# Between two attentions: another fixed order for routing and shared expert, and a shorter first lead in layer 1

## The chip, the cores and the metric

One Trainium2 chip, one of its cores. The time is the device time of one execution of the whole program in microseconds (us), the median of several runs; lower is better. The engines of the core run side by side, each through its own queue in order: TensorE (PE; PEld is its weight load), VectorE (DVE), ScalarE (ACT), GpSimd (POOL) and SyncE (SP, which issues most transfers).

## The reference, cut to what matters

2048 tokens of 128 channels, fp32, two layers, each with a modulated layer norm ahead of its attention and of its second half.

```python
h = layernorm(x) * (1 + ca) + sa
x = x + ga * attention0(h)            # 16 heads of 8, every token sees all 2048
h = layernorm(x) * (1 + cb) + sb
# 16 experts, the best one for each token, its score through a sigmoid,
# and a shared expert of width 512 for all tokens
x = x + gb * (down_e(silu(gate_e(s*h)) * up_e(s*h)) + shared_down(silu(h@G) * (h@U)))
h = layernorm(x) * (1 + ca1) + sa1
x = x + ga1 * attention1(h)           # 8 query heads of 16, one key/value head, causal
h = layernorm(x) * (1 + cb1) + sb1
x = x + gb1 * sigmoid(mix(h) @ Wr) * (relu(mix(h) @ Wk)**2 @ Wv)
```

## The kernel before, in words

Tokens are cut into 16 tiles of 128 and four blocks of 512 (`b` 0 to 3). `x` stays in SBUF with tokens on the partitions; the normed `h1` and `h2` lie transposed, channels on the partitions.

**Attention** (`attention`, both layers) works in units: one block of queries and one group of four heads, eight units in all. Each unit has two passes. The *first pass* computes scores for query tiles only to find the row maxima (TensorE L379, DVE L383, or L388 on the causal diagonal); a step is one query tile, one key block and two heads. `largest` packs the negated maxima, and `turn` transposes them (L412, copy L413). The *second pass* computes scores transposed (L444), adds the shift (L450, layer 1 only), takes the exponential on ScalarE (L454), clears what lies above the diagonal on POOL (L457) and weighs the values (L470). Three score tiles (`ps_s`) of two banks serve both passes. Two banks are left: one collects the weighed values, the other (`other_bank`) serves everything else, one piece after the other. `all_first` is a generator of all first-pass steps; `look_ahead(upto)` advances it. Before the first unit's second pass it runs `ends[0] + LEAD` steps, 16 in layer 1 (unit 0 and unit 1 have eight each), and afterwards stays eight steps and one unit's share ahead. In layer 1 the preparation of block b+1 (`ready1`: add the experts' rows and take moments, norm, turn, keys, values; then `project_q`, which ends in 16 transfers on SP's queue that stack the queries) starts at step 1 of the first unit of block b, one piece with each step. Unit 2 is the first that needs block 1. Within the attentions a planner sets each engine's order from its estimates of cost and from the order of the program.

**Between the attentions** (`last0` to `ordered.close()`) a manual schedule holds PE, DVE and ACT to the order in which the program issues their work; POOL and SP stay with the planner. `last0` returns the first list: the end of layer 0's attention for block 3 (`divide`, `turn_back`, `project`), the routing of block 3 (`moment`, `norm`, `turn`, `choose`, `place`, `turn_rows`, `send`; blocks 0 to 2 were routed inside the attention by the same `route`), the shared expert for block 0 in four slices (`up`, `times`, `down`, then `add`), and `tiles`, which computes on DVE which expert each of 31 slots of 128 rows belongs to. `send` scatters the scaled rows to DRAM with four indirect transfers from POOL (L759).

Then come the experts. SP reads the slots' start rows into registers and loads 31 tiles `xs` (L967) from what was scattered. Twelve *shared steps* (three blocks by four slices) remain: two products up (L941), Silu, a multiply (`acts`), and, one or two steps behind, a product down (L929). Eight *quads* of four slots run `gathered` (transpose xs, copy to `xsT`), `up_gate` (L1007, then `silu_up` into `acte`), `turn_act` (transpose, copy to `actT`) and `down` (L1020, then the multiply by gb L1024 and a write to `y_rows` from SP's queue, L1027). Pools: three `act` buffers shared by quads and shared steps, two `pg` tiles of two banks for `sg` and `gu`. Four shared steps run before the first quad, one in every second quad, four after. When all of `y_rows` is written, POOL gathers each token's row with 16 indirect transfers (L1044), addressed by `slot_i`.

At the head of layer 1 the pieces for block 0 follow all the shared work: add the gathered rows (L1062) and take moments, norm (L223), turn (L230, L231), keys (`stacked`, L265 to L267, `kS`), values and four stacked query products.

`moments` takes mean and variance per tile (L202, L203) and the inverse root by three Newton steps on DVE from a guess by shift (L205 to L217), so that ScalarE needs no other function table.

## Time and profile before

| | us |
|---|---|
| median of four runs (1273.35 to 1276.08) | 1275.21 |
| the profiled execution | 1275.1 |
| its span, first to last instruction | 1273.4 |
| layer 0's attention ends, the first list begins | about 817.5 |
| first shared up product of the experts' part | 847.18 |
| first quad's transposes | 857.74 |
| last quad's last product starts, then the last four shared steps | 901.84, 903.27 |
| last shared up product | 912.27 |
| first scores of layer 1 | 935.02 |
| first exponential of layer 1 | 962.43 |
| last product that weighs values | 1231.79 |

The mean granted TensorE clock is 0.935 of full. Over the span PE is busy 1168.1 us, DVE 946.9, ACT 774.1, POOL 95.2. All times below are from the start of the span. A stretch's row gives the busy time of each engine in it and how many instructions; a wait's row gives who waited, at which line, for whom, the sum, how often and the longest.

### The profile page before, as it was taken

How to read it: one execution, taken by the hardware profiler on the slowest of the kernel's cores; microseconds unless marked ns; L12 is line 12 of the kernel's file. 1: busy time of each engine (PE TensorE's matmuls, PEld its weight loads, DVE VectorE, ACT ScalarE, POOL GpSimd, SP SyncE). 2: the span in 40 equal slices, each digit the busy share in tenths (PEclk: the TensorE clock that was granted, in tenths of full speed). 3: DMA queues.
4: the chain of work that ended last, by engine and by line, in shares of the span. 5: the costliest groups of instructions: out<-in, count | busy, mean ns of one | idle time of the engine just before them, and what ended most of it. 6: DMA issues, size and time to landing. Idle time of an engine off the chain costs nothing.

```text
span 1273.4 us, 22384 instructions
## 1 busy us (share of the span) xinstructions
PE 1168.1 (92%) x9230; PEld 526.6 (41%) x9230; DVE 946.9 (74%) x1495; ACT 774.1 (61%) x843; POOL 95.2 (7%) x157
## 2 busy tenths in 40 slices
PE   5579999999999999999999999979768999999985
PEld 3233433443343343344344344447533444444432
DVE  3888898889889889898998881352467769888225
ACT  6107777777777777777777778613114435656763
POOL 2002000000000000000000000310311011100113
PEclk9658999999999999999999999979867779999998
DMA  4831010213122014010000000142201101000001
GB/s 120 114 47 34 2 52 1 68 33 86 52 68 68 2 47 121 2 51 2 2 2 2 2 1 6 40 124 60 58 11 33 34 1 35 1 2 1 1 2 33
DMA packets 63094, 45.22 MB, mean 36 GB/s; under 512 B 6608, under 2 KB 56912, under 8 KB 62480
## 3 DMA queue, kind: packets, MB, share of 16 engines
q1 hardware_dynamic: 60224, 40.37, 12.8%
q0 software_dynamic: 1024, 2.10, 0.6%
q10 hardware_dynamic: 1744, 1.32, 0.6%
q8 instruction: 73, 1.20, 0.4%
q14 instruction: 29, 0.24, 0.1%
HBM read 9.88 MB, written 21.95 MB: 25 GB/s over the span
## 4 chain that ended last, share of the span: by engine, by line
PE 81%; DVE 11%; ACT 4%; issue 2%; DMA 1%; POOL 1%; ACTq 0%; POOLq 0%; SPq 0%; DVEq 0%
PE a0bank L470 23%; PE a0p L444 17%; PE a0p L379 12%; PE a1bank L470 6%; PE a1p L444 4%; DVE a0mx L383 3%; PE a1p L379 2%; PE a1p L450 2%; DVE a1masked L388 2%; DVE a1mx L383 2%; PE sg L941 2%; ACT a0e L454 1%; PE gu L1007 1%; PE a1bank L265 1%; PE sum L929 1%
## 5 line engine op out<-in xcount | busy, mean ns | idle before, releaser
L383 DVE TENSOR_REDUCE a0mx<-a0p 128x2 f32<-128x1024 f32 x512 | 623.8, 1224 | 76.4 <-PE a0p L379 67.0
L454 ACT ACTIVATE a0e<-a0p 128x1024 f32<-128x1024 f32 x512 | 522.6, 1025 | 172.1 <-PE a0p L444 146.5
L470 PE MATMUL a0bank<-a0e,vA 128*32 128x256 f32 x4096 | 333.5, 392 | 0.2 <-ACT a0e L454 0.2
L379 PE MATMUL a0p<-kS,a0qS 64*128 64x512 f32 x1024 | 248.2, 481 | 24.7 <-DVE a0mx L383 13.4
L444 PE MATMUL a0p<-a0qS,kS 64*128 64x512 f32 x1024 | 260.5, 497 | 0.0
L454 ACT ACTIVATE a1e<-a1p 128x1024 f32<-128x1024 f32 (+3 forms) x160 | 143.2, 897 | 97.4 <-PE a1p L450 94.3
L444 PEld LDWEIGHTS a0p<-a0qS,kS 64*128 64x128 f32 x1024 | 97.3, 184 | 204.7 <-issue 128.4
L379 PEld LDWEIGHTS a0p<-kS,a0qS 64*128 64x128 f32 x1024 | 100.3, 192 | 109.3 <-ACT a0e L454 56.9
L470 PEld LDWEIGHTS a0bank<-a0e,vA 128*32 128x32 f32 x4096 | 86.4, 108 | 137.8 <-issue 124.7
L383 DVE TENSOR_REDUCE a1mx<-a1p 128x2 f32<-128x1024 f32 x96 | 115.8, 1222 | 28.6 <-PE a1p L379 27.7
L470 PE MATMUL a1bank<-a1e,vA 128*32 128x256 f32 (+1 forms) x1152 | 101.3, 385 | 2.3 <-POOL a1e L457 2.0
L444 PE MATMUL a1p<-a1qS,kS 64*128 64x512 f32 (+3 forms) x320 | 76.6, 471 | 2.8 <-DVE a1mx L388 0.9
L379 PE MATMUL a1p<-kS,a1qS 64*128 64x512 f32 (+3 forms) x320 | 68.8, 435 | 9.9 <-DVE a1mx L388 5.8
L388 DVE CUSTOM_DVE_ANT_0 a1masked<-a1p,later 128x128 f32<-128x128 f32 (+3 forms) x128 | 62.5, 488 | 12.1 <-PE a1p L379 7.1
L759 POOL DMA_INDIRECT sent<-hs,row_i x16 | 16.2, 1011 | 718.5 <-DVE ln11xn L223 689.9
L450 PE MATMUL a1p<-a1mT,a1ones 64*128 64x512 f32 (+3 forms) x320 | 62.1, 380 | 0.7 <-issue 0.7
L444 PEld LDWEIGHTS a1p<-a1qS,kS 64*128 64x128 f32 x320 | 31.6, 192 | 62.2 <-issue 33.2
L379 PEld LDWEIGHTS a1p<-kS,a1qS 64*128 64x128 f32 x320 | 33.1, 203 | 38.5 <-DVE a1mx L388 13.9
L457 POOL TENSOR_SCALAR_AFFINE_SELECT a1e<-a1e 128x256 f32<-128x256 f32 x64 | 26.3, 411 | 251.7 <-ACT a1e L454 251.7
L470 PEld LDWEIGHTS a1bank<-a1e,vA 128*32 128x32 f32 x1152 | 26.2, 109 | 45.8 <-issue 32.6
L413 ACT CAST a0mT<-a0bank 8x512 fp32r<-8x512 f32 x16 | 9.2, 576 | 45.1 <-PE a0bank L412 45.1
L450 PEld LDWEIGHTS a1p<-a1mT,a1ones 64*128 64x128 f32 x320 | 32.3, 197 | 2.3 <-issue 1.9
(342 smaller groups left out, 721.3 us busy)
## 6 DMA issues: line engine op xcount, KB each, us to landing
sent<-blank SPq DMA_DIRECT2D x68, 256.0 KB
kS<-a0qS SPq DMA_DIRECT2D x28, 128.0 KB
wgu_sb<-in_gate_up SPq DMA_DIRECT2D x1, 2048.0 KB
a0qS<-a0qh SPq DMA_DIRECT2D x62, 32.0 KB
a0qS<-a0ql SPq DMA_DIRECT2D x62, 32.0 KB
xs<-sent SPq DMA_DIRECT2D x31, 64.0 KB
y_rows<-y SPq DMA_DIRECT2D x7, 256.0 KB
a1qS<-a1qh SPq DMA_DIRECT2D x24, 64.0 KB
```

The source lines that it names most:

```text
L265: nc.tensor.matmul(ps, wS, h, start=True, stop=True)
L379: nc.tensor.matmul(ps[:, j, :n], qS[b][r:r + RT, st, i * P:(i + 1) * P], kS(st)[r:r + RT, kb * QB:kb * QB + n], start=True, stop=True)
L383: nc.vector.tensor_reduce(pm[:, i, 2 * pair:2 * pair + 2, kb], ps, AX.X, ALU.max)
L388: nc.vector.tensor_tensor_reduce(masked[:, :n], ps[:, j, :n], later[:, QB - n:], 1.0, LOWEST, ALU.add, ALU.max, pm[:, i, g, kb:kb + 1])
L444: nc.tensor.matmul(ps[:, j, q0:], kS(st)[r:r + RT, kt * P:(kt + 1) * P], qS[b][r:r + RT, st, q0:], start=True, stop=fused)
L450: nc.tensor.matmul(ps[:, j, q0:], ones[r:r + RT, g // S, :], shift[u][r:r + RT, q0:], start=False, stop=True)
L454: nc.scalar.activation(e[:, :, q0:], ps[:, :, q0:], AF.Exp, scale=scale)
L457: nc.gpsimd.affine_select(out=e[:, :, q0:q0 + P], in_=e[:, :, q0:q0 + P], compare_op=ALU.is_ge, fill=0.0, base=0, pattern=[[0, 2], [1, P]] ...
L470: nc.tensor.matmul(av[g * W:(g + 1) * W, c0:c1], vA(kt, grp * HG + g), held[kt, g // 2][:, g % 2, c0:c1], start=(kt == 0 and c0 == 0), sto ...
L759: nc.gpsimd.indirect_dma_start(out=sent[t], in_=hs[:, i, :], in_offset=None, out_offset=bass.IndirectOffsetOnAxis(ap=row_i.bitcast(U32)[:, ...
L929: nc.tensor.matmul(sums[b][:, i * P:(i + 1) * P], act[:, i * P:(i + 1) * P], wsd[:, k, :], start=(k == 0 and i == 0), stop=(k == NS - 1), ...
L941: nc.tensor.matmul(ps[:, j, :], w[:, k * P:(k + 1) * P], hT[:, b * QB:(b + 1) * QB], start=True, stop=True)
```

## The change

In `last0`, `divide` comes before the first `up`; Silu is a piece of its own; the moments' root is taken by ScalarE's Sqrt and a reciprocal on DVE, with `times(0)` between, and a one-column Sqrt ahead of it; `down(1)`, the rows and `place` follow `choose` directly; slices 2 and 3 come after `place`, their `times` and `down` after `tiles`; the running count (`ends_at`) is updated after `send`. In the experts' part three shared steps precede the quads (each with its down product as soon as one waits), three lie inside (quads 1, 3, 5) and six follow; each quad issues the next one's `gathered` first; `slot_i` is computed behind quad 2. At layer 1's head, add, norm and turn come after the last up product and the down product of the step before; the last multiply, keys, two queries, the last down product, values and two queries follow; the queries use the two-bank `pg` tiles; a one-column Exp is issued ahead. In layer 1's attention the first lead is 11 steps instead of 16 and grows back to eight ahead over unit 0's second pass, and block 1 is prepared from the first step of unit 1 (the other blocks as before).

```diff
...
-    def moments(b, name):
+    def moments(b, name, root=False, between=lambda: None):
...
         for i in range(TB):
             nc.vector.bn_stats(stats[:, i, :], x[:, b * TB + i, :])
             nc.vector.bn_aggr(mv[:, i, :], stats[:, i, :])
+        if root:
+            y = lnp.tile([P, TB], F32, name=name + "y", tag="y")
+            nc.scalar.activation(y, mv[:, :, 1], AF.Sqrt, bias=eps)
+            between()
+            nc.vector.reciprocal(y, y)
+            return mv, y
...
                             project_q(b + 1)
-                        if not fused and (grp, i) == (0, 1) and b + 1 < NB:
+                        if not fused and (grp, i) == (int(b == 0), 1 - int(b == 0)) and b + 1 < NB:
                             ready.extend(prepare(b + 1, other_bank))
                             ready.append(lambda b=b: project_q(b + 1))
...
-            look_ahead(ends[0] + LEAD)
+            short = 0 if fused else LEAD - 3
+            look_ahead(ends[0] + LEAD - short)
             for u in range(len(units)):
                 steps = second_pass(u)
                 size = ends[u] - (ends[u - 1] if u else 0)
                 more = ends[u + 1] - ends[u] if u + 1 < len(units) else 0
                 for n in range(1, size + 1):
                     next(steps)
-                    look_ahead(ends[u] + LEAD + more * n // size)
+                    lead = LEAD - (short * (size - n) // size if u == 0 else 0)
+                    look_ahead(ends[u] + lead + more * n // size)
                     if n == size:
                         next(steps, None)
...
             nc.vector.tensor_copy(row_i[:, ts], row[:, ts])
+            if not parts:
+                nc.vector.tensor_tensor(at[b + 1], at[b], ps[:, TB, :], ALU.add)
+            return ps
+
+        def ends_at(ps):
             nc.vector.tensor_tensor(at[b + 1], at[b], ps[:, TB, :], ALU.add)
...
         if parts:
-            return ([lambda: got.extend(moments(b, f"ln1{b}")),
+            return ([lambda between: got.extend(moments(b, f"ln1{b}", True, between)),
                      lambda: got.append(normal(b, f"ln1{b}", *got)),
                      lambda: turn_normal(bank(), got[2], h1[:, cols], m[:, 4:5], m[:, 3:4]),
-                     choose], place, turn_rows, send)
+                     choose], place, ends_at, turn_rows, send)
...
         total = third[:, 0, :]
-        (moment, norm, turn, choose), place, turn_rows, send = route(NB - 1, bank, parts=True)
+        (moment, norm, turn, choose), place, ends_at, turn_rows, send = route(NB - 1, bank, parts=True)
...
         def up(k, j):
             ps = banks[k % 2]
             nc.tensor.matmul(ps[:, j, :], (wsg, wsu)[j][:, k * P:(k + 1) * P],
                              h1[:, HOFF:HOFF + QB], start=True, stop=True)
-            if j == 0:
-                tile_of[k] = ep.tile([P, 2, QB], F32, name=f"s0act{k}", tag="e")
-                nc.scalar.activation(tile_of[k][:, 0, :], ps[:, 0, :], AF.Silu)
+
+        def silu(k):
+            tile_of[k] = ep.tile([P, 2, QB], F32, name=f"s0act{k}", tag="e")
+            nc.scalar.activation(tile_of[k][:, 0, :], banks[k % 2][:, 0, :], AF.Silu)
...
+        def table(func):
+            nc.scalar.activation(lnp.tile([P, 1], F32, name="s0table", tag="table"), eps, func)
         made = []
-        return [lambda: up(0, 0), divide, lambda: up(0, 1), turn_back, lambda: times(0),
-                lambda: up(1, 0), project, moment, lambda: up(1, 1), lambda: down(0),
-                lambda: up(2, 0), lambda: up(2, 1), norm, turn, lambda: times(1),
-                lambda: times(2), choose, lambda: up(3, 0),
-                lambda: made.append(turn_rows(third[:, 1, :])), lambda: down(1),
-                lambda: down(2), lambda: place(), lambda: up(3, 1), lambda: send(made[0]),
-                lambda: times(3), tiles, lambda: down(3), add]
+        def rows():
+            made.append(turn_rows(third[:, 1, :]))
+        return [divide, lambda: up(0, 0), lambda: silu(0), turn_back, lambda: up(0, 1), project,
+                lambda: up(1, 0), lambda: silu(1), lambda: up(1, 1), lambda: table(AF.Sqrt),
+                lambda: moment(lambda: times(0)), lambda: down(0), norm, turn,
+                lambda: times(1), choose, lambda: down(1), rows, lambda: made.append(place()),
+                lambda: up(2, 0), lambda: silu(2), lambda: send(made[0]), lambda: ends_at(made[1]),
+                lambda: up(2, 1), lambda: up(3, 0), lambda: silu(3), lambda: up(3, 1), tiles,
+                lambda: times(2), lambda: down(2), lambda: times(3), lambda: down(3), add]
...
-        def silu_up(ps, n, name):
-            g, up = ps
+        def silu(g, n, name):
             sig = wp.tile([P, n], F32, name="sig" + name, tag="sig")
+            v = sig if len(g.shape) == 2 else sig.rearrange("p (j f) -> p j f", f=P)
+            nc.scalar.activation(v, g, AF.Silu)
+            return v
+        def times(v, up, n, name):
             act = wp.tile([P, n], F32, name="act" + name, tag="act")
-            v = [t if len(g.shape) == 2 else t.rearrange("p (j f) -> p j f", f=P)
-                 for t in (sig, act)]
-            nc.scalar.activation(v[0], g, AF.Silu)
-            nc.vector.tensor_tensor(v[1], v[0], up, ALU.mult)
+            w = act if len(up.shape) == 2 else act.rearrange("p (j f) -> p j f", f=P)
+            nc.vector.tensor_tensor(w, v, up, ALU.mult)
             return act
...
         def shared_act(b, k, ps):
-            waiting.append((b, k, silu_up((ps[:, 0, :], ps[:, 1, :]), QB, f"s{b}{k}")))
+            v = silu(ps[:, 0, :], QB, f"s{b}{k}")
+            return lambda: waiting.append((b, k, times(v, ps[:, 1, :], QB, f"s{b}{k}")))
         def shared_step():
             up = shared_up()
             if waiting:
                 shared_down()
-            shared_act(*up)
+            shared_act(*up)()
...
-        first = [shared_up() for _ in range(2)]
-        for up in first:
-            shared_act(*up)
-        for n in range(2):
+        for n in range(3):
             shared_step()
-        here = rp.tile([P, NE], F32, name="here")
-        nc.vector.tensor_tensor(here, base, at[0], ALU.subtract)
-        slots = rp.tile([P, NT, NE], F32, name="slots")
-        nc.vector.tensor_tensor(slots, mine.bitcast(F32),
-                                here.unsqueeze(1).to_broadcast([P, NT, NE]), ALU.mult)
-        slot = rp.tile([P, NT], F32, name="slot")
-        nc.vector.tensor_reduce(slot, slots, AX.X, ALU.add)
-        nc.vector.tensor_tensor(slot, slot, row, ALU.add)
-        slot_i = rp.tile([P, NT], I32, name="slot_i")
-        nc.vector.tensor_copy(slot_i, slot)
         regs = registers(1, mybir.EngineType.PE, NE - 1)
...
-            acts[q] = silu_up((ps[:, :n, :P], ps[:, :n, P:]), n * P, f"e{q}")
+            acts[q] = times(silu(ps[:, :n, :P], n * P, f"e{q}"), ps[:, :n, P:], n * P, f"e{q}")
...
+        slot_i = rp.tile([P, NT], I32, name="slot_i")
+        def slots_of_tokens():
+            here = rp.tile([P, NE], F32, name="here")
+            nc.vector.tensor_tensor(here, base, at[0], ALU.subtract)
+            slots = rp.tile([P, NT, NE], F32, name="slots")
+            nc.vector.tensor_tensor(slots, mine.bitcast(F32),
+                                    here.unsqueeze(1).to_broadcast([P, NT, NE]), ALU.mult)
+            slot = rp.tile([P, NT], F32, name="slot")
+            nc.vector.tensor_reduce(slot, slots, AX.X, ALU.add)
+            nc.vector.tensor_tensor(slot, slot, row, ALU.add)
+            nc.vector.tensor_copy(slot_i, slot)
         gathered(0)
         for q in range(len(quads) + 2):
+            if q + 1 < len(quads):
+                gathered(q + 1)
             if q < len(quads):
                 up_gate(q)
             if q >= 2:
                 down(q - 2)
-            if q + 1 < len(quads):
-                gathered(q + 1)
-            if q % 2 == 0 and q < len(quads):
-                shared_step()
             if 1 <= q <= len(quads):
                 turn_act(q - 1)
+            if q in (1, 3, 5):
+                shared_step()
+            if q == 2:
+                slots_of_tokens()
...
-        pieces = ready1(0, bank)
-        values = pieces.pop()
-        for st in range(4):
-            pieces.append(lambda st=st: stacked(bank(), wq1s[:, st, :], h2[:, :QB], 0,
-                                                tmp[(st + 1) % 2], qS1[:, st, :]))
-        pieces.insert(-2, values)
-        for n in range(len(shared)):
+        add, norm, turn, keys, values = ready1(0, bank)
+        pairs = {}
+        def queries(st):
+            if st % 2 == 0:
+                pairs[0] = pg.tile([P, 2, QB], F32, name=f"qs{st}", tag="g")
+            stacked(pairs[0][:, st % 2, :], wq1s[:, st, :], h2[:, :QB], 0, tmp[(st + 1) % 2],
+                    qS1[:, st, :])
+        while len(shared) > 1:
             shared_step()
-        while waiting:
-            shared_down()
-        for piece in pieces:
-            piece()
+        up = shared_up()
+        shared_down()
+        last_times = shared_act(*up)
+        nc.scalar.activation(rp.tile([P, 1], F32, name="a1table"), eps, AF.Exp)
+        add()
+        norm()
+        turn()
+        last_times()
+        keys()
+        queries(0)
+        queries(1)
+        shared_down()
+        values()
+        queries(2)
+        queries(3)
         ordered.close()
     attention(1, h2, H1 // HG, D1, float(P) ** -0.5, True, pool1,
```

## The prediction

> **What bounds it now.** The page's chain of what ended last comes first: it is TensorE's (81%), so I cut the span at the change and ask what TensorE does there. Columns: stretch, its length, busy time (instructions) of PE, PEld, DVE, ACT, POOL, granted clock, DMA share, GB/s.
>
> ```profile
> PE 81%; DVE 11%; ACT 4%; issue 2%; DMA 1%; POOL 1%; ACTq 0%; POOLq 0%; SPq 0%; DVEq 0%
> 817.50:847.20 29.70, 20.31 (x106) 12.69 (x102) 16.55 (x59) 6.37 (x10) 5.95 (x9) 0.83 0.39 116
> 847.20:857.70 10.50, 10.50 (x32) 5.44 (x33) 2.08 (x4) 2.39 (x4) 0.00 (x0) 0.83 0.33 91
> 857.70:903.30 45.60, 40.52 (x237) 32.97 (x237) 14.67 (x26) 15.71 (x28) 0.00 (x0) 0.98 0.22 64
> 912.30:935.00 22.70, 13.79 (x50) 7.26 (x49) 11.06 (x34) 4.81 (x7) 13.11 (x14) 0.77 0.15 38
> 935.00:963.10 28.10, 18.95 (x60) 9.59 (x60) 21.47 (x102) 4.59 (x6) 1.27 (x1) 0.52 0.07 17
> 963.10:1232.30 269.20, 257.85 (x2197) 119.82 (x2196) 180.93 (x392) 155.35 (x184) 28.84 (x66) 0.94 0.04 11
> ```
>
> Before 817, and once the lead is equal again, the change edits nothing. Up to 847 and from 912 to 963 TensorE is idle a third of the time or more, and half-clocked in parts; from 847 to 912 it is nearly full; from 963 it bounds layer 1. Next the timeline and the waits:
>
> ```profile
> 818.17 1.28 ACT L852 ACT_TABLE_LOAD   x1
> 846.45 0.67 DVE L867 TENSOR_TENSOR x<-x,s0ps 128x512 f32<-128x512 f32 x1
> 847.18 2.08 PE L941 MATMUL sg<-hT,wsg_sb 128*128 128x512 f32 x2 [4.61 <-DVE x L867]
> ...
> DVE acte L921 <- PE sum L929: 15.3, 3, 5.5
> ...
> PE gu L1007 <- ACT xsT L997: 1.6, 4, 0.7
> PE gu L1007 <- DVE acte L921: 1.5, 3, 0.5
> PE y_ps L1020 <- DVE y L1024: 1.4, 1, 1.4
> PE y_ps L1020 <- ACT actT L997: 0.6, 1, 0.6
> ...
> 917.31 0.68 DVE L1062 TENSOR_TENSOR x<-x,yx 128x512 f32<-128x512 f32 x1
> 922.28 1.12 DVE L223 TENSOR_SCALAR ln20xn<-x,ln20mv,ln20y 128x128 f32<-128x128 f32 x4
> 922.68 1.25 PE L230 MATMUL a1bank<-ident,ln20xn 128*128 128x128 f32 x4 [6.01 <-DVE ln20xn L223]
> 961.14 1.28 ACT L454 ACT_TABLE_LOAD   x1 [0.97 <-PE a1p L450]
> ```
>
> See four places: the shared expert waits for the last0 list's closing add; expert activations wait for a shared down product; layer 1's first norm runs after all products; the exponential's table arrives when wanted.
>
> **1. The list after layer 0.** The route's chain. Now ten DVE instructions (827.00 to 829.40, 2.4 us) form the root; after: a root of four columns on ScalarE (0.20 as topsig's, 0.31 as the 16 columns of L182), a reciprocal (0.25) and, between, times(0) (0.69, formerly in a DVE gap). First `up(0,0)` behind divide frees `a0o` of a Silu (0.25 earlier). ScalarE then has silu(1) to 825.65, the root's table to 826.95, a dummy call, root by 827.4; DVE's aggregates end at 826.7. Norm at 827.65 instead of 829.40: 1.75. Place stood behind up(3,0), the rows and two down products (833.64 to 838.38, 4.7); it now has one down product and the rows before it, so it starts near 834.4 instead of 838.38 and the first scatter on POOL near 836.7 instead of 841.04. The tile arithmetic (841.27 to 846.53, 5.3) ends near 842.0.
>
> But the list still ends in times(2), times(3), down(2), down(3), add, all behind that arithmetic on DVE: 842.0 + 0.7, down(2) and down(3) after some 4 us of idleness at half clock (2 x 0.89 x 1.24/0.66, the transposes at L230 cold and warm: 3.4), 0.25 to the add, 0.7: 847.05 against 847.12. Gain 0.1; bounds -1.5 (place late) to +2 (products warm). `ends_at` is 0.16 on DVE behind the scatter's multiply. What does come 4.3 earlier is the list of tiles: SP's 31 `xs` loads start at 844.9 instead of 849.18, the first quad's four land by 849.4 at worst; TensorE reads them at 854. Nothing waits for that, before or after.
>
> Extra tables cost one or two loads of 1.28 (root's, then one for Tanh and Silu); after the load at 818.17 the Silu began 0.01 later. The root's lies beside bn_stats and times(0). The second, if it comes only once Tanh's input is there (832.2), makes topsig ready at 833.9, before place's sums want DVE near 834.9. On the path they cost 0 to 2.6; I take 0, as both covers are in the rows. The Trainium skill, "ScalarE: Activation LUTs", What ACT_TABLE_LOAD costs, asks 1.28 plus a drain, about 2.66 per switch, which speaks against this root. By it norm would start near 829, the step would gain 0.4 instead of 1.75; no drain stands in the trace, so the row decides.
>
> **2. Shared steps and quads.** A shared step is 1.72 (ups) + 0.89 (down). From the first up (847.18) to the last up (912.27): 65.1. Before the quads: 4 steps with two downs, 6.9 + 1.8, and 1.9 of half clock (ups of 2.08 and 1.84). After: 3 steps, 5.2 + 1.8 = 7.0; the clock is warm because down(2), down(3) work just ahead. That is my choice; if not, +1.9. Quads, 857.74 to 903.27, 45.5: 4 shared steps 10.4; the quads' own products 0.45 + 1.72 + 0.87 + 0.43 = 3.47 for each of 7.75, 26.9; so 8.2 are stalls. Causes: `gathered(q+1)` is issued just before its product (xsT's copy), and three `act` buffers, one held by a waiting shared product, stop acte for 5 us. After: gathered comes a round early; the order e, e, s lets each buffer be free a round before reuse. Stalls: 0.8 at the first quad, 2.5 in the tail (copy, product, multiply, with nothing beside). 26.9 + 3 x 2.61 + 3.3 = 38.0. Bounds for stalls: 2.5 to 8.2. Then five whole steps before the last up, 13.05 + 1.0 cold. Sum 7.0 + 38.0 + 14.05 = 59.0: **6.1 gained**; the last up starts near 906.1 instead of 912.27.
>
> `slots_of_tokens` (0.17, 0.42, 0.42, 0.17, 0.17) moves behind the third quad, on a DVE that is a third busy; POOL needs it 25 us later. The last expert write then leaves near 892.9; POOL's gathers start 3.3 later as now (904.08 to 907.37), four take 5.0, landing 2 to 5: 903 to 906. The add (L1062) stands on DVE at 906.5 with norm, last_times and all queued behind it; late gathers would cost their lateness. I take 0.
>
> **3. Layer 1's head.** Now last up to first score (935.02): 22.75. After, add and norm run on DVE beside the last up and a down: last up + 0.45 (the preceding times) + 4.97 (917.31 to 922.28) + 0.4 + 1.25 (transposes) + 0.85 (hT) = 8.0. From hT to the last query now 10.2 (924.75 to 934.97); queries in the wide banks need no wait for a copy, while last_times, a down (0.89) and an add (0.68) come between: 9.4. 17.45: **5.3 gained**, bounds 3 to 7. The Exp load goes beside DVE work.
>
> **4. The lead.** 16 first-pass steps ran before a second pass; now 11, and block 1's preparation starts after unit 0's. Unit 0's maxima took 935.39 to 945.87 (10.5) with that preparation in their gaps; alone 8.6. The first exponentials come at about S+12 (S the first score) instead of S+27.4 (962.43). Against this block 1's norm comes at S+16.8 instead of S+11.5 (946.51), and the chain from it (transposes, keys, values, queries, SP's stacking issues, 1.2 a pair) to unit 2's first maximum took 17.4 (to 963.94): S+34.2 instead of S+28.9. Loss 5.3. In the hole TensorE does second-pass scores: a unit's scores, shift rows and weights are 2.2 each (two pairs, widths 512 to 128, 0.215 per product of 512), 13.2 for units 0 and 1, 0.8 a score. Two readings. If TensorE bounds from unit 2 on: four scores ahead and the 1.28 load off the path, -5.3 + 3.3 + 1.3 = -0.7. If DVE bounds there: unit 2's second pass must await its maxima (8 x 1.22 + 8.6 = 18.4, block 2's preparation 6.5), S+59, where now TensorE is still in unit 1 to 999, S+64: +5, and about +9 if unit 2 isn't late. I take **+1**, nearer the first, because three score banks let the second pass run only a few scores past a waiting unit 2. Ends -14.7 (rival c) and +9.
>
> **Sum.** 0.1 + 6.1 + 5.3 + 1 = 12.5. The profiled execution took 1275.1 (span 1273.4), 0.1 under the median 1275.21: 1262.7.
>
> **Rivals.** (a) *Quads no better:* stalls stay 8.2 and the ups cold: 12.5 - 4.9 - 1.9 = 5.7, 1269.5. For: the tail's waits and the shared pools remain. Against: the buffer count above. (b) *Lead pays fully:* +9 instead of +1, 1254.7. For: half clock of 0.52 at 935 to 963. Against: stacking is late. (c) *Slower: block 1's preparation.* If three scores get between keys, values and queries on TensorE's queue at their present spacing (957.48 to 963.70 to 967.93, some 4.2), unit 2 starts at S+34.2 + 12.6, 17.9 late, of which four scores (3.2) are done: -14.7, and 1275.2 - 11.5 + 14.7 = 1278.4. It decides above 14 lost. For: TensorE takes its queue in order. Against: the present order lets ready scores pass waiting pieces (L444 at 957.48 ahead of a blocked L412). (d) *Nothing reaches the end:* the earlier places serve loads that nobody waits for, as step 1 says; with steps 2 to 4 cancelling, 1275.
>
> **Chances.** Forecast, 1258 to 1267: 0.48. (a) 0.20. (b) 0.15. (c) 0.11. (d) 0.06. A difference of 0.2% (2.6 us) is about what can be told from none. Faster 0.83, same 0.06, slower 0.11. The range 1253 to 1274 leaves out the lower part of (b), all of (c) and half of (d), together under 0.2.
>
> **What would show it.** L867 still ending near 847; no Newton steps in ln13, and `xs` issues by 845; TensorE's waits at L1007 under 1 us; the last y product near 892; ln20xn's transposes soon after 911, first score near 923.5; first a1e 12 us later; unit 2's first L383 34 us after it. Wrong: gathers that hold L1062, a half clock past 850, or unit 2 later than 40.

## The result

The changed kernel takes 1277.03 us in the median of 49 runs (1268.45 to 1288.28), the kernel before 1274.22 in 74 runs beside it: 1.0034 of before, 95% interval 1.0024 to 1.0045. It is slower by 4 us, where 12.5 us of gain was forecast, and lies above the range. A few executions in a slower state, the one of 1288.28 among them, are left out of the ratios and of the clock figures below.

First the stretches, as they were shown of before, in the profile of the changed kernel (1268.46 us, span 1266.7, at the fast end of its runs). Columns: stretch, length, busy time (instructions) of PE, PEld, DVE, ACT, POOL, granted clock, DMA share, GB/s. The lines of the code have moved: L967 is now L993, L1062 is L1089, L223 is L230, L383 is L390, L444 is L451, L454 is L461.

```profile
PE 81%; DVE 10%; ACT 4%; issue 1%; DMA 1%; POOL 1%; SPq 0%; ACTq 0%; POOLq 0%; DVEq 0%
817.50:845.60 28.10, 19.86 (x110) 12.18 (x102) 15.04 (x48) 10.82 (x15) 5.69 (x9) 0.94 0.43 129
845.60:853.10 7.50, 7.28 (x29) 4.08 (x30) 1.85 (x3) 1.79 (x3) 0.00 (x0) 1.00 0.45 127
853.10:891.00 37.90, 36.31 (x224) 30.79 (x225) 14.21 (x26) 15.12 (x27) 0.00 (x0) 1.00 0.25 72
903.40:925.50 22.10, 13.31 (x44) 6.26 (x43) 11.16 (x34) 6.30 (x9) 9.88 (x12) 0.78 0.12 30
925.50:962.40 36.90, 24.79 (x106) 12.72 (x106) 22.91 (x102) 6.89 (x9) 2.90 (x5) 0.55 0.04 11
962.40:1224.10 261.70, 246.82 (x2151) 115.74 (x2150) 180.62 (x391) 151.91 (x178) 26.92 (x62) 0.95 0.05 12
```

Up to the first score the gain is there: it comes at 925.52 where it came at 935.02, 9.5 us earlier (the forecast said 923.5). The quads' stretch is TensorE's almost without a gap at full clock. The loss lies behind: from the first score to the first maximum of unit 2 it is now 36.9 us at a clock of 0.55, where it was 28.9. And this profile flatters the kernel: a typical run of it is 8 to 10 us longer. A second profile of the same kernel, taken on another chip (1278.7 us, span 1277.0), has its first score at 928.56, so that 6.5 us are left of the gain up to there, and then:

```profile
928.60:965.60 37.00, 24.82 (x106) 12.50 (x106) 22.93 (x103) 6.89 (x9) 2.90 (x5) 0.55 0.04 11
965.60:1234.70 269.10, 256.11 (x2150) 120.31 (x2150) 180.78 (x391) 151.82 (x178) 26.91 (x62) 0.91 0.05 11
```

The same 2150 products take 269.1 us instead of 261.7. The other engines are busy for the same time within 0.2 us; what differs is the clock, 0.91 against 0.95. So every run below has a second number beside its time: its *half-clock time*, 2 x (1 - clock) x span. This counts the clock as either half or full; no stretch shown here has less than 0.50. Its median is 184 us in the changed kernel (152 to 205 over the runs) and 155 to 163 in the kernel before. Within the runs of one kernel, time goes with it by 0.25 to 0.47 us for each us in every edited kernel that has six runs or more (0.33 in the changed one, correlation 0.96), and by 0.12 to 0.40 in the kernel before.

### The profile page after: what moved, and what is told of

Read it like the earlier page. It is cut to its first block, busy times and chain, and to the rows that moved or that the text cites. A ratio compares the mean times of both kernels' runs of the same rounds, so it can differ in the third digit from the quotient of the medians.

```text
span 1266.7 us, 22371 instructions
## 1 busy us (share of the span) xinstructions
PE 1158.7 (91%) x9230; PEld 523.7 (41%) x9230; DVE 946.7 (75%) x1484; ACT 778.8 (61%) x849; POOL 94.2 (7%) x157
## 3 DMA queue, kind: packets, MB, share of 16 engines
q1 hardware_dynamic: 60224, 40.37, 13.1%
## 4 chain that ended last, share of the span: by engine, by line
PE 81%; DVE 10%; ACT 4%; issue 1%; DMA 1%; POOL 1%; SPq 0%; ACTq 0%; POOLq 0%; DVEq 0%
PE a0bank L477 24%; PE a0p L451 17%; PE a0p L386 12%; PE a1bank L477 5%; PE a1p L451 4%; DVE a0mx L390 3%; PE a1p L386 3%; PE a1p L457 2%; DVE a1masked L395 2%; DVE a1mx L390 2%; PE sg L966 2%; ACT a0e L461 1%; PE gu L1018 1%; ACT a1e L461 1%; PE a0bank L508 1%
## 5 line engine op out<-in xcount | busy, mean ns | idle before, releaser
L390 DVE TENSOR_REDUCE a0mx<-a0p 128x2 f32<-128x1024 f32 x512 | 623.8, 1224 | 76.2 <-PE a0p L386 66.8
L461 ACT ACTIVATE a0e<-a0p 128x1024 f32<-128x1024 f32 x512 | 522.6, 1025 | 172.0 <-PE a0p L451 146.5
L451 PE MATMUL a0p<-a0qS,kS 64*128 64x512 f32 x1024 | 260.5, 497 | 0.0
L461 ACT ACTIVATE a1e<-a1p 128x1024 f32<-128x1024 f32 (+3 forms) x160 | 143.2, 897 | 100.3 <-PE a1p L457 97.0
L451 PEld LDWEIGHTS a0p<-a0qS,kS 64*128 64x128 f32 x1024 | 97.3, 184 | 204.7 <-issue 128.8
L390 DVE TENSOR_REDUCE a1mx<-a1p 128x2 f32<-128x1024 f32 x96 | 115.8, 1222 | 26.2 <-PE a1p L386 25.4
L477 PE MATMUL a1bank<-a1e,vA 128*32 128x256 f32 (+1 forms) x1152 | 97.8, 387 | 2.1 <-DVE a1ql L251 1.7
L451 PE MATMUL a1p<-a1qS,kS 64*128 64x512 f32 (+3 forms) x320 | 76.6, 466 | 3.5 <-ACT a1e L461 1.3
L451 PEld LDWEIGHTS a1p<-a1qS,kS 64*128 64x128 f32 x320 | 31.9, 192 | 61.0 <-issue 35.3
```

The source lines that it names most:

```text
L390: nc.vector.tensor_reduce(pm[:, i, 2 * pair:2 * pair + 2, kb], ps, AX.X, ALU.max)
L451: nc.tensor.matmul(ps[:, j, q0:], kS(st)[r:r + RT, kt * P:(kt + 1) * P], qS[b][r:r + RT, st, q0:], start=True, stop=fused)
L461: nc.scalar.activation(e[:, :, q0:], ps[:, :, q0:], AF.Exp, scale=scale)
L477: nc.tensor.matmul(av[g * W:(g + 1) * W, c0:c1], vA(kt, grp * HG + g), held[kt, g // 2][:, g % 2, c0:c1], start=(kt == 0 and c0 == 0), sto ...
```

## The experiments

Twelve kernels besides the change itself, some of them two or three times, on five chips; each ratio is to the runs of the kernel before on the same chip. The names e1 to e19 are the beginnings of the runs' labels. "S" is the first score of layer 1. All of them compute the whole reference.

| run | what | ratio, 95% interval | half-clock us, median |
|---|---|---|---|
| e17 | before + list alone | 0.9957 [0.9940, 0.9975] | 138 |
| e18 | before + shared steps alone | 0.9946 [0.9926, 0.9966] | 147 |
| e8, e15, e19 | before + both | 0.9998 [0.9977, 1.0019], 0.9890 [0.9864, 0.9916], 0.9896 [0.9871, 0.9922] | 163, 141, 137 |
| e1, e12, e14 | and the new head (change without its lead) | 0.9931, 0.9931, 0.9919 (each +-0.002) | 153, 157, 147 |
| after, e13 | and the lead: the whole change | 1.0034 [1.0024, 1.0045], 1.0033 [1.0005, 1.0060] | 184, 187 |

**The lead put back, alone, and in halves (one chip).** The first edit, on the changed kernel:

```diff
-                        if not fused and (grp, i) == (int(b == 0), 1 - int(b == 0)) and b + 1 < NB:
+                        if not fused and (grp, i) == (0, 1) and b + 1 < NB:
...
-            short = 0 if fused else LEAD - 3
+            short = 0
```

> The changed kernel with layer 1's lead and the start of block 1's preparation as before; everything between the attentions stays changed. Theory L (late preparation: unit 2's first pass waits for block 1's queries) and theory T (thin second pass: the early, sparse second pass of units 0 and 1 holds TensorE at half clock): first score near 925.5, first maximum of unit 2 near 954.5 (29 us after it, as before), time 1264 to 1267, that is 9.5 us under the kernel before. Theory S (something in the new order between the attentions slows layer 1): 1273 to 1278.

Measured 1264.36 us, 0.9931 [0.9911, 0.9951]; S at 923.98, unit 2's first maximum at S+27.4, half-clock time 153. The other three steps together are worth 8.8 us; against the 1277.03 of the result, which did not run beside it, the lead costs about 12.6. The second kernel is before with these two places alone as the change has them:

> The kernel before with only the lead and the start of block 1's preparation changed. Theories L and T: first score at 935 as before, unit 2's first maximum near 972 (37 us after it), time 1284 to 1288, some 12 us over the kernel before. Theory S: 1272 to 1276, no difference.

Measured 1277.6, 1.0030 [1.0009, 1.0050]: slower, but by 3.8 us, not 10 or more. Unit 2 comes at S+38.0; the half-clock time is 159 in the median with two clusters near 153 and 185. So the lead's price depends on the kernel that it is put into: 12.6 us on one that has 153 us at half clock, 3.8 on one that already has some 160. Why is not shown. The two halves, first the short lead with block 1 prepared as before (e3), then the full lead with block 1 prepared late (e4):

> The changed kernel with the short first lead (11 steps) but block 1's preparation from step 1 of unit 0 as before. Theory L: unit 2's first maximum 29 to 31 us after the first score, 1262 to 1267, no worse than the one with both taken back. Theory T: the second pass is as early and thin as in the changed kernel, so 1273 to 1279.

> The changed kernel with the full first lead (16 steps) but block 1's preparation from the first step of unit 1. Theory L: unit 2's first maximum 37 us or more after the first score, 1275 to 1283, as the changed kernel or worse. Theory T: 1264 to 1268, as with both taken back.

Short lead: 1273.42, 0.9994 [0.9970, 1.0018], 9.1 us above e1, unit 2 at S+32.0, half-clock time 181. Late preparation: 1270.63, 0.9982 [0.9967, 0.9998], 6.3 us above e1, unit 2 at S+36.5, half-clock time 159. So the lateness of unit 2 belongs to the preparation, and most of the additional half-clock time to the short lead. Each costs time; together they cost 12.6, less than their sum. The profiles, one of each, agree: over the 40 us from unit 2's first maximum on, the clock is 0.59 with the short lead alone and 0.73 and 0.61 in the two profiles of the whole change, but 0.90 with the late preparation alone and 0.87 with both put back. Theory T's reason does not fit, though: with the short lead alone the first exponential comes at S+27.2, as late as before the change (S+27.4), so an early second pass is not what holds the clock down in that profile.

**Preparation by twos (e11).** If the late norm were what makes unit 2 late, taking two pieces at a step would mend it (the expectation says "full lead": the changed kernel's own growing lead is meant).

```diff
-                        if ready:
-                            ready.pop(0)()
+                        for _ in range(2 if not fused and b == 0 else 1):
+                            if ready:
+                                ready.pop(0)()
```

> The changed kernel with block 1's preparation taken two pieces at a step of the first pass, not one: add and norm at one step, turn and keys at the next, values and queries at the third. Nothing else differs, the full lead stays. If late preparation is what the lead costs, the norm comes at about S+16 (S: the first score) in place of S+21.7, the stacking transfers some 6 us earlier, unit 2's first maximum at S+30 to S+32 in place of S+36.9, and the time falls by 5 to 12 us, to about 0.994 to 0.999 of before. If only the half clock counts, and it comes from VectorE's maxima standing ahead of everything that keeps TensorE busy, the time stays within 3 us of the changed kernel's and its half-clock time with it.

Measured 1275.79, 1.0010 [0.9990, 1.0031], half-clock time 173: 3 us better than the changed kernel beside it, the two intervals overlap. The norm came 3.5 us earlier (S+18.2), and unit 2 not at all (S+38.7). The timeline of this kernel shows why; S is 924.95:

```profile
943.17 1.11 DVE L230 TENSOR_SCALAR ln21xn<-x,ln21mv,ln21y 128x128 f32<-128x128 f32 x4
945.68 2.07 PE L272 MATMUL a1bank<-hT,wk_sb 128*128 128x512 f32 x2 [0.87 <-ACT hT L238]
949.41 1.09 PE L419 MATMUL a1bank<-ident,a1nm 128*128 128x128 f32 x4 [1.04 <-DVE kS L274]
951.17 1.91 PE L1099 MATMUL a1bank<-wv_sb,hT 128*128 128x32 f32 x8 [0.68 <-ACT a1mT L420]
953.74 2.07 PE L357 MATMUL a1bank<-hT,wq_sb 128*128 128x512 f32 x2
956.47 0.69 DVE L251 TENSOR_TENSOR a1ql<-a1bank,a1qh 128x512 fp32r<-128x512 f32 x1 [3.05 <-ACT a1qh L250]
963.64 2.36 DVE L390 TENSOR_REDUCE a1mx<-a1p 128x2 f32<-128x1024 f32 x2 [4.09 <-PE a1p L386]
```

Norm to last cast is 13.3 us: keys, the turn of unit 1's maxima, values and queries go through one bank, one after the other, each product 2.07 at half clock, and then 7.2 us until the stacked queries are there and scored. In the changed kernel norm to maximum is 15.2 us, here 20.5: what the earlier norm gained was lost again behind it. The add of block 1's rows did not move, at S+10.5 (935.45) behind all of unit 0's maxima on DVE. And the test is not a clean one, since the first exponential moved from S+14.0 to S+29.0.

**Scores twice (e6).** A test of the other cause: the first-pass scores of units 0 to 2 of layer 1 are issued twice, so that TensorE stands idle less.

```diff
-                        nc.tensor.matmul(ps[:, j, :n], qS[b][r:r + RT, st, i * P:(i + 1) * P],
-                                         kS(st)[r:r + RT, kb * QB:kb * QB + n],
-                                         start=True, stop=True)
+                        for twice in range(2 if causal and u <= 2 else 1):
+                            nc.tensor.matmul(ps[:, j, :n], qS[b][r:r + RT, st, i * P:(i + 1) * P],
+                                             kS(st)[r:r + RT, kb * QB:kb * QB + n],
+                                             start=True, stop=True)
```

> The changed kernel with every first-pass score product of layer 1's units 0 to 2 issued twice into the same place: more TensorE work, nothing else. Theory T (half clock through sparse work is what most of the lost time is): half-clock time of a run falls from 184 us (median) to 160 or less and the time from 1277 to 1268 to 1273, though work is added. Theory L (lateness of block 1's queries alone): half-clock time may fall, the time is 1277 to 1281.

Measured 1283.6, 1.0040 [1.0020, 1.0060], half-clock time 169 (164 to 180). The half-clock time went down against the changed kernel's 184, taken on other chips; the time did not, and unit 2 came at S+39.7. Theory T's 1268 to 1273 did not come. Keeping TensorE busy by force is no remedy here, and this run can't tell the clock's share from the added work.

**The same comparison on another chip, and the clock within one kernel.**

> The changed kernel with the lead and the start of block 1's preparation put back, on another chip and beside the changed kernel itself. On the first chip it stood at 0.9931 of before (1264.4 us), on the second the same kernel with a wide tile for each query at 0.9928. If the first three steps of the change are worth what those two runs say, it stands at 0.992 to 0.995 again, and 10 to 13 us below the changed kernel of this same call. If it was a matter of the chip, it is over 0.997. Half-clock time (2 x (1 - clock) x span) about 153 us if the tie of time and clock holds.

> The changed kernel itself, on this chip, as the other end of the same comparison: 1.001 to 1.005 of before, about 1277 to 1281 us, with its half-clock time at 175 to 185 us in the median, some 30 us above the kernel with the lead put back. If the loss of the lead is lateness alone, its half-clock time is within 10 us of that kernel's and its time is still 12 us longer.

0.9931 [0.9908, 0.9954] and 1.0033 [1.0005, 1.0060], medians 1267.71 and 1279.47, half-clock time 157 and 187. Taking the mean of the runs, 13.1 us lie between them with 32 us of half-clock time; with both brought to 160 us by the slope of all of this chip's runs (0.30), 3.6 remain, and by the slope of these two kernels alone (0.35) 1.9. The runs of the result and e1, not taken side by side, stand at 1270.6 and 1268.0 at 160 us. The halves divide in the same way: at 160 us the late preparation alone is 4.4 us above e1, the short lead alone 0.8. So 2 to 4 us go with unit 2's lateness and some 9 to 11 with the half clock; lateness alone, which had the half-clock times within 10 us of each other, is refuted. That is a tie, not yet a cause; for the cause, the two profiles of the changed kernel. The program is one and the same. At 976 and 979 they run 3.13 us apart (3.04 at the first score). Then, in the timeline of the profile of 1268.46 us:

```profile
984.40 0.90 PE L386 MATMUL a1p<-kS,a1qS 64*128 64x512 f32 x4
986.38 1.08 PE L1098 MATMUL a1bank<-wv_sb,hT 128*128 128x32 f32 x8
992.58 1.07 PE L477 MATMUL a1bank<-a1e,vA 128*32 128x256 f32 x16 [0.18 <-DVE a1ql L251]
...
1034.95 1.13 PE L357 MATMUL a1bank<-hT,wq_sb 128*128 128x512 f32 x2
1040.43 0.33 PE L508 MATMUL a1bank<-ident,a1o 128*128 128x128 f32 x1
```

and in that of 1278.7:

```profile
987.74 1.53 PE L386 MATMUL a1p<-kS,a1qS 64*128 64x512 f32 x4
990.04 1.91 PE L1098 MATMUL a1bank<-wv_sb,hT 128*128 128x32 f32 x8
997.24 1.93 PE L477 MATMUL a1bank<-a1e,vA 128*32 128x256 f32 x16
...
1044.24 2.07 PE L357 MATMUL a1bank<-hT,wq_sb 128*128 128x512 f32 x2
1050.96 0.33 PE L508 MATMUL a1bank<-ident,a1o 128*128 128x128 f32 x1
```

The same products take 1.53 for 0.90, 1.91 for 1.08, 1.93 for 1.07, 2.07 for 1.13. The distance grows from 3.1 to 4.7 (at 997.24) and 10.5 (at 1050.96), and at the end of the attention it is 10.6. The stretches around 1038 say the same, first of the shorter execution, then of the longer one:

```profile
1026.00:1032.00 6.00, 5.68 (x24) 2.48 (x23) 3.35 (x5) 1.74 (x3) 1.67 (x2) 0.72 0.00 0
1032.00:1038.00 6.00, 5.61 (x40) 2.77 (x38) 3.17 (x5) 3.44 (x4) 0.00 (x0) 1.00 0.01 3
1038.00:1044.00 6.00, 6.00 (x44) 2.90 (x46) 5.75 (x14) 2.86 (x5) 0.00 (x0) 1.00 0.00 0
```

```profile
1032.00:1038.00 6.00, 6.00 (x19) 2.46 (x21) 2.56 (x3) 1.28 (x3) 1.67 (x2) 0.50 0.00 0
1038.00:1044.00 6.00, 6.00 (x26) 3.15 (x24) 2.20 (x3) 1.49 (x2) 0.00 (x0) 0.50 0.01 3
1044.00:1050.00 6.00, 6.00 (x28) 2.65 (x28) 2.74 (x7) 3.20 (x4) 0.00 (x0) 0.65 0.00 0
```

While block 3 is prepared, the clock falls; in one execution it is back within some 3 us, in the other after some 17, though TensorE has work all the time. So within one program the clock alone moves the end by 7.5 us; that much is shown. Why the short lead has more half-clock time is not: the runs tie the two together, but none held the rest fixed and changed the clock.

**The head of layer 1.** The queries of one pair share a wide tile. One kernel (e5) gives each query a wide tile of its own, with the lead put back:

```diff
-            if st % 2 == 0:
-                pairs[0] = pg.tile([P, 2, QB], F32, name=f"qs{st}", tag="g")
-            stacked(pairs[0][:, st % 2, :], wq1s[:, st, :], h2[:, :QB], 0, tmp[(st + 1) % 2],
+            pairs[0] = pg.tile([P, 2, QB], F32, name=f"qs{st}", tag="g")
+            stacked(pairs[0][:, 0, :], wq1s[:, st, :], h2[:, :QB], 0, tmp[(st + 1) % 2],
```

> The kernel with layer 1's lead as before (median 1264.4), and each of the four head queries in a wide tile of its own instead of two in one. If the shared tile makes the second query's product wait for the first one's copy (16.91 after 16.11 in the changed kernel's trace): from hT to the last query 9.4 to 10.2 us instead of 13.9, first score near 920, time 1259 to 1262. If the copies on ScalarE and VectorE set the pace in any case: 13 to 14 us and 1263 to 1266.

and one (e8) undoes the head whole (all shared steps, their downs, then the pieces), with the lead put back, which is before with the list and the shared steps:

> The kernel with layer 1's lead as before (median 1264.4), and in addition the head of layer 1 as before (norm after all products, queries in narrow tiles, the exponential's table loaded when wanted). By the prediction's step 3 the head is worth 5.3: 1268 to 1271. By the rows of the profiles (22.1 from the last up to the first score instead of 22.9): 1264 to 1266.5.

On this chip: 0.9928 [0.9901, 0.9955] and 0.9998 [0.9977, 1.0019], the old head 0.0070 or 9 us worse than the tiles of their own. From hT's end to S it is 10.1 us with those tiles (920.00 to 930.10) and was 14.0 in the changed kernel, 14.8 in e1: the shared tile is what the second query of a pair waits for. That this is worth anything at the end of the kernel is not shown: 0.9928 is no better than e1's 0.9931 with shared tiles on another chip, and the 1259 to 1262 did not come. And every one of the four kernels run on this chip has a stop in this stretch that no kernel on the other chips has, for instance in the timeline of the first:

```profile
912.65 0.60 ACT L937 ACTIVATE sigs<-sg 128x512 f32<-128x512 f32 x1 [7.75 <-issue]
919.22 0.78 ACT L238 ACTIVATE hT<-a1bank,mod 128x512 f32<-128x512 f32 x1 [4.46 <-remote]
```

ScalarE stands for 7.75 us ahead of the last Silu, where 2.01 is usual, behind nothing that the profile shows. In two others it is 6.45 and 9.63, put down there to the norm and to its transposes; in the one with the old head DVE stands for 9.26, again behind nothing shown. From the last up product to hT's end the old head takes 21.2 us here and 11.7 in e15 and e19, the three new heads 13.9 to 14.2 where 7.1 to 7.2 is usual, so by these profiles the stop weighs some 2.7 us more on the old head; that leaves some 6 of the 9 us. So the head was compared again on a fourth chip (e14, e15):

> The changed kernel with the lead and the start of block 1's preparation put back, as the yardstick for the two next runs: 0.991 to 0.995 of before, first score at 924 to 932 us.

> The same with the old head of layer 1 (all shared steps, then all downs, then add, norm, turn, keys, queries). On the second chip this cost 0.0067 of the time, some 8.5 us, but in its profile the add stood 9.2 us behind nothing that the profile shows, and every kernel on that chip had a stop of 6 to 10 us in the same stretch. If the stop is the chip's and not the old head's, the rows price the new head at 0.8 us (22.9 against 22.1 us from the last shared up to the first score), and the ratio stands 0.000 to 0.002 above the yardstick. If the old head costs what it did, 5 us or more, it stands 0.004 to 0.008 above.

0.9919 [0.9899, 0.9938] with the new head, 0.9890 [0.9864, 0.9916] with the old: the old head is no worse, rather 2.9 us better, with intervals that overlap. The rows fit. With the new head (first fence, S at 929.09) the norm is early and the queries wait; with the old (second, S at 928.21) it is 4.1 us later and the queries pass:

```profile
911.73 1.12 DVE L230 TENSOR_SCALAR ln20xn<-x,ln20mv,ln20y 128x128 f32<-128x128 f32 x4
913.47 0.78 ACT L238 ACTIVATE hT<-a1bank,mod 128x512 f32<-128x512 f32 x1 [3.24 <-PE a1bank L237]
919.64 2.08 PE L272 MATMUL qs<-hT,wq1s_sb 128*128 128x512 f32 x2 [1.56 <-DVE a1qS L274]
926.40 1.13 PE L272 MATMUL qs<-hT,wq1s_sb 128*128 128x512 f32 x2 [1.62 <-DVE a1qS L274]
```

```profile
915.82 1.12 DVE L230 TENSOR_SCALAR ln20xn<-x,ln20mv,ln20y 128x128 f32<-128x128 f32 x4
917.50 0.78 ACT L238 ACTIVATE hT<-a1bank,mod 128x512 f32<-128x512 f32 x1 [9.23 <-PE a1bank L237]
924.66 1.98 PE L272 MATMUL a1bank<-hT,wq1s_sb 128*128 128x512 f32 x4
```

**The list.** The old list in the kernel with the lead put back, on two chips:

> The kernel with layer 1's lead as before (median 1264.4), and in addition the list after layer 0 as before (its Newton root, places late, slices in the old order); quads and head stay changed. By the prediction's step 1 the list is worth 0.1: 1263 to 1266. By the rows of the profiles (first shared up at 843.2 to 845.6 with the new list, 846.1 to 847.2 with the old, and three ups at full instead of half clock behind it): 1267 to 1270.

> The yardstick with the old list between the attentions. By the rows (21.9 us from the norm's first statistics to the first tile's shared product with the old list, 18.9 to 20.6 with the new) it costs 1.3 to 3.0 us, 0.001 to 0.0025 above the yardstick; the second chip's 0.0040 would be the upper end. By the prediction's +0.1 it would be level with the yardstick.

0.9971 [0.9948, 0.9995] (e7) and 0.9969 [0.9950, 0.9989] (e16): the second is 0.0050 above its yardstick, 6 us; the first has none on its chip and is 0.0040 above e1. Then the root alone, back on VectorE (e10, with the lead put back and without the one-column Sqrt):

```diff
-        if root:
-            y = lnp.tile([P, TB], F32, name=name + "y", tag="y")
-            nc.scalar.activation(y, mv[:, :, 1], AF.Sqrt, bias=eps)
-            between()
-            nc.vector.reciprocal(y, y)
-            return mv, y
+        between()
```

> The kernel with the lead put back, and in its list between the attentions the root of the norm back on VectorE in its steps of 0.17 to 0.19 us, and no table load for a root on ScalarE. The prediction put the root on ScalarE at nothing on the path that ends the list, because the gathers' places and not the norm were late there. By that: within 2 us of the kernel with the lead put back. By the rival, that the norm's 2 us on VectorE sit ahead of everything that the list does next: first expert tile's shared product 2 to 3 us later than 843.2 us, and the time 2 to 4 us longer.

0.9963 [0.9942, 0.9984], where the same kernel with the root from ScalarE had 0.9931 beside it: 4 us by the ratios, 1.7 by the medians, and the intervals overlap. From the norm's first statistics to the first shared up of the experts' part it is 22.4 us with this root, 18.9 (e1) or 20.6 (e12, e14) with ScalarE's, and with the whole old list 21.9 in the kernel before, 20.9 to 22.6 in others (e2, e16, e7). So by these rows what the list gained in its own stretch is the root, and the new order by itself gained nothing there; e10 is one profile.

**Each step alone.**

> Before with only the new list between the attentions (places first, the root from ScalarE). By the rows it ends 1.3 to 3.0 us earlier, counted from the norm's first statistics; by the prediction 0.1. If that is all that reaches the end: 0.9976 to 0.9999 of before. If the new list is worth what taking it out cost (0.0050 in the third comparison): 0.995.

> Before with only the second step: half of the shared expert behind the quads, three shared steps ahead, the places of the tokens later. The rows say 7.0 us from the first tile's shared product to the last; the prediction said 6.1. If they reach the end: 0.994 to 0.996 of before. If the head of layer 1 gives them back (its gathers go out later and the last tile's add waits for them): 0.998 to 1.000.

> The first two steps together, with the old head and the old lead: 0.989 of before in the third comparison, with an interval of 0.9864 to 0.9916. If the steps add up, it stands at the sum of the two runs beside it, 0.988 to 0.992; if it was the draw of six runs, at 0.992 to 0.995.

List alone 1267.02, 0.9957 [0.9940, 0.9975]; shared steps alone 1265.34, 0.9946 [0.9926, 0.9966]; both 1260.70, 0.9896 [0.9871, 0.9922]. They add up (0.9957 x 0.9946 = 0.9903), and both together without the new head and without the lead are the best version found on two chips, 13 us ahead of before, and 17 to 18 ahead of the change by their ratios. On the third, in e8, the same kernel was level with before (0.9998, with the stop described above), so the 13 us did not come everywhere. The list's 5.5 us are more than the 1.3 us of its rows: its half-clock time is 138 us where before has 160 beside it. In its profile the stretch from the last quad's last product to the last pair of ups runs at full clock (9.46 us for 11.13) and unit 2's maximum comes at S+27.2 for S+28.9. The shared steps alone: 847.94 to 908.70 for the first up to the last pair, where before has 847.18 to 912.97, 5.0 us less. Where the first up comes at full clock, as in the changed kernel's first profile and e1, it is 58.7.

## Why the prediction was wrong

It forecast 12.5 us; the four steps, as factors, are 0.9957 (e17) x 0.9946 (e18) x 1.0029 (e14 over e15) x 1.0103 (e13 over e12) = 1.0034. The last two are quotients on the way to the whole change, so the product has to come out near the result; what it shows is that the first two add.

*Step 4, the lead: wrong, and the step that turned a gain into a loss.* It was taken at +1 between ends of -14.7 and +9, nearer the reading in which TensorE bounds from unit 2 on. Measured: -13. Two terms failed. The loss from block 1's late preparation was put at 5.3 us on unit 2's place (S+34.2 instead of S+28.9) and was 8.0 (S+36.9). And the clock of TensorE had no term in the sum: it was taken as given in each stretch. In the rows of the changed kernel (S is 925.52) the lateness arises ahead of the norm, on VectorE:

```profile
936.16 0.69 DVE L1089 TENSOR_TENSOR x<-x,yx 128x512 f32<-128x512 f32 x1
938.73 0.16 DVE L212 TENSOR_SCALAR ln21v<-ln21mv 128x4 f32<-128x4 f32 x1
947.02 0.16 DVE L224 SCALAR_TENSOR_TENSOR ln21y<-ln21t,ln21y 128x4 f32<-128x4 f32 x1
947.23 1.29 DVE L230 TENSOR_SCALAR ln21xn<-x,ln21mv,ln21y 128x128 f32<-128x128 f32 x4
962.45 1.23 DVE L390 TENSOR_REDUCE a1mx<-a1p 128x2 f32<-128x1024 f32 x1 [4.15 <-PE a1p L386]
```

The add comes at S+10.6, behind unit 0's maxima. The steps of the root, 2.4 us one after the other in the list before, are spread over 8.5 us between unit 1's maxima, of which the reckoning says nothing, and the norm comes at S+21.7 instead of S+16.8. From the norm to unit 2's first maximum it is 15.2 us, less than the 17.4 reckoned. So rival (c), scores between keys, values and queries on TensorE's queue, did not occur: its 1278.4 lies near the measured 1277.03 by luck. The sign that the prediction gave for a wrong lead, unit 2 later than S+40, did not appear either.

At equal half-clock time lateness is worth only 2 to 4 of the 13 us. The rest goes with the half clock, 30 us more of it in the median of the runs. The row that hinted at it was there, 0.52 from 935 to 963, and was used only for a rival that gains. That the clock moves the end of one program by 7.5 us is shown; why the short lead brings more half-clock time stays open. "First a1e 12 us later" nearly held (S+14.0): the exponentials start early and then stand still again from 947 to 965. Of the rivals, (a) and (b) failed: the quads lost their stalls, and the lead cost. (d) failed too: a gain reached the end wherever the lead was put back, except in e8.

The other steps' misses offset each other by luck: the list gained 5 us more than forecast, and the head 5 us less or worse.

*Step 3, the head: the norm right, the queries wrong.* The add and norm went as worked out: 8.1 us from the last up to hT's end (8.0 forecast), no wait for the gathers, the table of the exponential beside DVE's work. "Queries in the wide banks need no wait for a copy" failed: 14.0 instead of 9.4, since two queries share one tile and the second waits for the copy of the first (1.56 and 1.62 in the rows above, and the chain behind them). That ate the gain: 5.3 forecast; nothing on the fourth chip, where the old head was if anything 2.9 us better. On the chip with the stops the old head lost 9 us to a head with tiles of their own; how much of that is the head stays open.

*Step 2, shared steps and quads: right.* 57.9 us from first to last up, 59.0 forecast; the quads' stretch 36.55 to its last product, without the waits for a shared product; the last y at 889.6 (892 forecast). Alone it is worth 6.9 us at the end of the kernel by the ratio, 6.1 forecast. Whether TensorE is warm ahead of the quads, which was a choice there, changes from run to run: from the first up to the quads it is 7.5 us in one profile of the changed kernel, 9.9 in the other.

*Step 1, the list: a term missed.* It gained 0.1 by the forecast, because the tile arithmetic on DVE, and not the norm, was thought to stand ahead of the last products. In fact the norm's 1.5 us (2.63 us after the first statistics instead of 4.11) came through to the end of the list, by the rows of the experiment with the root; in its time this is within the intervals. Alone the list is worth 5.5 us at the end (e17), of which its own stretch explains 1.3. The list of tiles came early as argued (SP's loads from 843.35 instead of 849.18) and nothing waited for it, as argued. "Table loads cost 0" held, though there are three more of them and not one or two (825.99, 830.26, 831.95): the root's load stands at 825.99 for 1.28 and the root at 827.39, beside DVE's statistics. First the norm before, then the changed kernel's rows:

```profile
829.40 1.11 DVE L223 TENSOR_SCALAR ln13xn<-x,ln13mv,ln13y 128x128 f32<-128x128 f32 x4
```

```profile
825.99 1.28 ACT L887 ACT_TABLE_LOAD   x1
827.28 0.20 ACT L887 ACTIVATE s0table<-eps 128x1 f32<-128x1 f32 x1
827.39 0.28 ACT L207 ACTIVATE ln13y<-ln13mv,eps 128x4 f32<-128x4 f32 x1
827.71 0.18 DVE L209 RECIPROCAL ln13y<-ln13y 128x4 f32<-128x4 f32 x1 [0.17 <-ACT ln13y L207]
827.92 1.12 DVE L230 TENSOR_SCALAR ln13xn<-x,ln13mv,ln13y 128x128 f32<-128x128 f32 x4
```

The Trainium skill, "ScalarE: Activation LUTs", What ACT_TABLE_LOAD costs, gives about 2.66 us for a switch, a drain included; here no more than the 1.28 can be seen, with the next activation 0.01 us behind the load.

## What to carry to other kernels

Price each part of a change by itself against the end of the kernel: here two parts gained 13 us together on two chips of three, one gained nothing that could be shown and one took it all back, and the sum alone would have thrown out the good with the bad. Where a stretch of the profile shows a clock of 0.5, how long TensorE stays at half clock is a cost of its own, and an edit can go with more of it well behind the place where it was made; read the granted clock of every run, not of one profile. And when products get a wider tile so that they need not wait, see that no two of them share it.

## What was not expected of the hardware

The changed kernel's runs spread from 1268 to 1286 us on one program, and this goes with the granted clock at a correlation of 0.96. The Trainium skill, "TensorE: Matmul & The Clock Gate", Part 1, says that a window of about 3.4 us of work releases the clock, that this window runs free of the program, and that the ramp costs under 1% of a typical span. The free phase fits a program whose clock differs from run to run. The window's length does not: from 1032 to 1044 the longer execution shows TensorE busy 6.00 of 6 us twice at a clock of 0.50, more than three such windows (as far as a modelled busy time can say it). The 1% is for one ramp; here the clock falls again and again, and the spread of the half-clock time alone, 53 us at 0.33, is worth 1.4% of the span.

The stop of 6 to 10 us on ScalarE or VectorE near 905 to 919 came in the profiles of all four kernels on one chip and in none on the others; POOL's gathers were being issued then (896 to 916 in e5), as on the other chips too (895 to 915 in the changed kernel). What it waited for stays open.
